# Node features loaded on 128 partitions in halves and quarters, and the node table stored in blocks of 512 nodes

## The chip, the cores and the metric

The kernel runs on one core of a Trainium2 chip. The metric is the device time of one launch in microseconds. The core has five instruction streams that matter here: PE (matrix products; PEld is its weight load), DVE (vector operations), ACT (activations and copies, and some DMA issues), POOL (GpSimd: here mostly DMA issues whose descriptors it writes itself, the indirect gathers among them) and SP (DMA issues only). Sixteen DMA engines move the data of all queues.

## The reference, cut to what matters

One layer of a graph network, with 12500 nodes of 160 features, 400000 edges sorted by destination, and a layer norm at the end. The 160 features of a node are 64 scalars and 32 vectors of 3 components.

```python
s = x[:, :64]; v = x[:, 64:].reshape(n, 32, 3); a = node_vec1
h_s = s @ lin1_ws * a / sqrt(64)                              # first maps: the table
h_v = einsum('nci,cd->ndi', v, lin1_wv) * a[:, :, None] / sqrt(32)
w = silu(edge_attr_64 @ fc_w1 / sqrt(64)) @ fc_w2 / sqrt(64)  # weights of an edge
es, ev = h_s[src], h_v[src]                                   # gather from the table
# products of es, ev with w and with edge_attr_4 (e0, e1): mid_s, mid_v
agg = segment_sum(mid, dst, n) / sqrt(16)
o = agg @ lin2 * a                                            # second maps
pre = self connection of x (sc_ws, sc_wv) + o
x = layernorm(x + gated(pre))
```

The change concerns the two lines of the first maps alone: how `x` comes into the core, how `h` is computed from it, and how `h` gets into the table in DRAM from which the edges gather.

## The kernel before, in words

The host lays the inputs out: `xs_t` is the 64 scalar features transposed (64 rows of 12500 nodes), `xv_t` the 96 vector components (three groups of 32 rows), `attr` the node attribute as 128 partitions by 98 columns (node = 128 x column + partition). The order of the instructions on each engine is that of the program (a manual schedule); engines wait for one another by semaphores only.

The start (lines 203 to 383). First come constants: an identity, iotas, memsets. `share`, an iota of 1040 numbers on POOL (L219), is needed only by `bases`, which derives the first node of each block of edges from the first row of `dst`. Then the node features are loaded in chunks of CH = 2048 nodes by `load` on SP (L233): `xa` holds the scalars in partitions 0 to 63 (L239) and two of the three vector components in 64 to 127 (L240), each a DMA of 64 rows of 8 KB; `xz` holds the third component (L245), as quarters: partition 4 c + q has component row c, quarter q of the chunk, so that 128 partitions hold 512 nodes each. There are six full chunks and a last one of 212 nodes. Between the loads ACT issues those of the weights, of the attribute (`at`, L265) and of the first row of `dst` (L268).

From the weights two matrices of 128 x 128 are built on DVE: `l1` has the scalar map and two copies of the vector map on its diagonal, `l1z` the vector map four times, spread so that rows of one quarter feed the columns of that quarter.

The loop over the chunks (L320): per chunk 16 matmuls (L331) turn 128 nodes each into 128 of the 160 features, with the features as the stationary operand; four at a time fill a PSUM bank (`hp`). DVE multiplies a bank with the attribute into `ht` (L334). Four more matmuls (L347) and one DVE product (L350) make the last 32 features of all 2048 nodes. After the fourth chunk begins, `bases` runs once on DVE (L309). At the end of a chunk POOL issues one DMA that stores 2048 rows of 640 bytes to the table `h_tab` (L361). `ht` has three buffers, so the fourth chunk's products wait for the first chunk's store. A matmul of fp32 shows as two records of PE.

After the loop: `lo` spreads the bases over the partitions with PE (L371). POOL issues, behind its stores, the edge features of the first chunk of edges (`es`, two DMAs, L372) and the whole of `dst` (`dt`, L373). SP issues, behind the last 84 rows' store (L364), the small weights of the later maps (L386, L297, L409), and then what the edge loop loads. When `dt` is there, DVE computes `rel`, each edge's destination less its block's base (L416, L421). Its PSUM is then free for the banks of the edge loop.

The edge loop (L874) takes 4 tiles of 128 edges a step, 3125 tiles in all. POOL gathers the source rows of each tile from `h_tab` with one indirect DMA (L468) into one of four buffers of four tiles (44 tiles are fetched by SP, row by row). PE computes the hidden layer (L459) and the weights of the edges (L510), DVE the products (L520, L528), PE sums them up by destination (L589), and further steps turn, map and add the sums. A buffer of gathered rows is free when the products of its step are done.

## Time and profile before

| | |
|---|---|
| median of 3 runs | 3964.24 us (3958.78 to 3966.85) |
| the profiled execution: its own time | 3954.57 us |
| its span | 3952.6 us |
| PE busy | 3649.2 us (92%) |
| POOL busy | 2929.3 us (74%) |
| DVE busy | 2415.6 us (61%) |
| ACT busy | 894.0 us (23%) |
| DMA traffic | 412.50 MB, 104 GB/s in the mean, 230 GB/s in the first of 40 slices |

The page gives the whole execution; the change lies in its first fortieth. So the useful answers are those for a window: the windows view gives for a stretch of time the busy time and the number of instructions of PE, PEld, DVE, ACT and POOL, the granted PE clock, the mean busy share of the DMA engines and their rate in GB/s. A line of the timeline has the start and the duration in us, engine, line, operation, what it writes and reads, how many instructions were merged, and in brackets how long the engine had been idle and what released it. In the list of groups stand the busy time and the mean in ns, and then the idle time before the group with its releasers. In the list of waits stand the total in us, how often, and the longest. A releaser is inferred, and where several were awaited it is the one that came last by the trace.

### The profile page before, as it was taken

The page shows a single profiled execution, that of the slowest core. Times are in us where ns is not written, and L with a number is a line of the kernel's source. Part 1 is how long each engine was busy: PE and PEld are TensorE (multiplying, and loading weights), DVE is VectorE, ACT ScalarE, POOL GpSimd, SP SyncE. Part 2 cuts the span into 40 slices and gives each one's busy share as a digit, 9 for nine tenths or more (in the row PEclk, how much of TensorE's full clock was granted, in tenths as well). Part 3 has the DMA queues.
Part 4 walks back from the last instruction along what each step waited for, and adds up shares of the span by engine and source line. Part 5 has one row for each costly group of instructions (what it writes and reads, how often), then busy time and mean ns, then how long its engine had stood idle before and what let it go on. Part 6 is the DMA issues. An engine that isn't in the chain of part 4 may idle for free. (4 is left out here: it accounts for less than half of the span.)

```text
span 3952.6 us, 58252 instructions
## 1 busy us (share of the span) xinstructions
PE 3649.2 (92%) x14269; PEld 1584.2 (40%) x14269; DVE 2415.6 (61%) x6524; ACT 894.0 (23%) x2480; POOL 2929.3 (74%) x3100
## 2 busy tenths in 40 slices
PE   5899999999999999999999999999999998999997
PEld 4343343343444344334344344344343443344343
DVE  5656565665665665656656656666665665666665
ACT  1322222222222222222222222222221221222222
POOL 4777777777777777777777777777777777777774
PEclk8999999999999999999999999999999999999999
DMA  8443444444444444344443443444443444444442
GB/s 230 97 103 90 108 105 96 108 103 105 100 96 110 103 97 108 95 116 96 102 110 86 110 110 89 108 100 100 108 106 90 109 103 105 100 100 108 100 109 55
DMA packets 243192, 412.50 MB, mean 104 GB/s; under 512 B 83069, under 2 KB 173497, under 8 KB 241945
## 3 DMA queue, kind: packets, MB, share of 16 engines
q0 software_dynamic: 150160, 262.93, 27.3%
q1 hardware_dynamic: 92246, 145.66, 15.8%
q8 instruction: 115, 1.88, 0.2%
q14 instruction: 235, 1.93, 0.2%
q10 hardware_dynamic: 436, 0.10, 0.0%
HBM read 392.43 MB, written 16.00 MB: 103 GB/s over the span
## 5 line engine op out<-in xcount | busy, mean ns | idle before, releaser
L468 POOL DMA_INDIRECT hg<-h_tab,idx x3081 | 2915.0, 946 | 949.5 <-issue 846.7
L510 PE MATMUL pw<-w,hid 128*128 128x448 f32 x3126 | 1363.3, 560 | 119.1 <-DVE sel L582 78.2
L589 PE MATMUL pa<-pr,sel 128*64 128x416 f32 x6250 | 1302.2, 539 | 3.1 <-DVE pw L573 2.9
L528 DVE TENSOR_TENSOR pr<-pw,hg 128x384 f32<-128x384 f32 x2313 | 1136.9, 547 | 0.0
L520 DVE TENSOR_TENSOR pr<-pw,hg 128x512 f32<-128x512 f32 x771 | 532.7, 691 | 876.8 <-DMA hg<-h_tab,idx 623.1
L510 PEld LDWEIGHTS pw<-w,hid 128*128 128x128 f32 x3126 | 555.2, 194 | 595.2 <-issue 461.6
L589 PEld LDWEIGHTS pa<-pr,sel 128*64 128x64 f32 x6250 | 388.0, 139 | 814.0 <-issue 803.6
L795 ACT COPY sa<-pa 128x416 f32<-128x416 f32 x521 | 263.3, 505 | 1205.7 <-PE pa L589 1190.5
L573 DVE TENSOR_TENSOR pw<-rel,iota 128x64 f32<-128x64 int16 x782 | 179.6, 230 | 543.5 <-PE pw L510 541.2
L459 PE MATMUL misc<-es,w 128*128 128x512 f32 (+1 forms) x784 | 450.2, 656 | 26.8 <-DVE rel L421 21.6
L461 ACT ACTIVATE hid<-misc 128x512 f32<-128x512 f32 x392 | 233.5, 596 | 778.4 <-PE misc L459 778.1
L598 PEld LDWEIGHTS misc<-ident,sa 128*128 128x128 f32 x2084 | 240.2, 141 | 318.7 <-issue 267.8
L613 PE MATMUL misc<-tt,l 128*96 128x256 f32 (+5 forms) x1474 | 343.6, 380 | 6.6 <-DVE y L659 6.0
L598 PE MATMUL misc<-ident,sa 128*128 128x128 f32 x2084 | 328.4, 280 | 8.3 <-DVE acc L776 3.8
L582 DVE TENSOR_TENSOR sel<-pw,eas 128x256 f32<-128x256 f32 x782 | 322.8, 413 | 0.0
L613 PEld LDWEIGHTS misc<-tt,l 128*96 128x96 f32 (+1 forms) x1474 | 225.2, 162 | 142.5 <-issue 73.9
L601 ACT COPY tt<-misc 128x192 f32<-128x192 f32 x521 | 164.7, 316 | 501.9 <-PE misc L598 482.6
L459 PEld LDWEIGHTS misc<-es,w 128*128 128x128 f32 x784 | 119.6, 192 | 293.8 <-issue 238.5
L621 DVE TENSOR_TENSOR acc<-acc,os 96x32 f32 x1042 | 194.6, 187 | 28.0 <-ACT os L616 9.6
L646 PE MATMUL misc<-ident,acc 96*128 96x96 f32 x196 | 36.6, 272 | 97.1 <-DVE pw L573 67.9
L603 ACT COPY tt<-misc 128x64 f32<-128x64 f32 x521 | 117.1, 225 | 0.0
L616 ACT COPY os<-misc 96x512 f32<-96x512 f32 (+2 forms) x67 | 38.2, 569 | 293.4 <-PE misc L613 286.7
(86 smaller groups left out, 608.6 us busy)
## 6 DMA issues: line engine op xcount, KB each, us to landing
es<-in_es_t_dram SPq DMA_DIRECT2D x258, 384.0 KB
hq<-h_tab SPq DMA_DIRECT2D x5632, 0.6 KB
hg<-h_tab,idx POOLq DMA_INDIRECT x3081
h_tab<-ht POOLq DMA_DIRECT2D x6, 1280.0 KB
xt<-in_x_dram SPq DMA_DIRECT2D x23, 320.0 KB
out_dram<-y SPq DMA_DIRECT2D x23, 320.0 KB
xv<-in_xv_t_dram SPq DMA_DIRECT2D x25, 187.5 KB
xs<-in_xs_t_dram SPq DMA_DIRECT2D x25, 125.0 KB
```

Of the source, the lines that this page charges most:

```text
L459: nc.tensor.matmul(ph[:k, c], w1[:k, :k], es[:k, t0 * P + c0 * P:t0 * P + c1 * P], start=True, stop=True)
L461: nc.scalar.activation(hid[:k, c], ph[:k, c], AF.Silu, scale=1.0 / math.sqrt(64))
L468: nc.gpsimd.indirect_dma_start(out=hg[:, t, :], out_offset=None, in_=h_tab, in_offset=bass.IndirectOffsetOnAxis(ap=i, axis=0))
L510: nc.tensor.matmul(pw[:, t:t + m, :NWT], hid[:m * S, c * P:(c + 1) * P], w2[:m * S, :m], start=True, stop=True)
L520: nc.vector.tensor_mul(two, pw[:, :n, :2 * S].rearrange("p t (k c) -> p t k c", k=2), hg[:, :n, None, :S].to_broadcast([P, n, 2, S]))
L528: nc.vector.tensor_mul(pr[:, :n, first:first + V3].rearrange("p t (i c) -> p t i c", i=3), pw[:, :n, None, 2 * S + k * V:2 * S + (k + 1) * ...
L582: nc.vector.tensor_mul(sel[:, :n], oh[:, :, None, :].to_broadcast([P, n, 4, W]), by_slot(tiles[0][0])[:, u:u + n, :, None].to_broadcast([P ...
L589: nc.tensor.matmul(pa[half * ROWS:(half + 1) * ROWS, :NPR], sel[:, t].rearrange("p k w -> p (k w)"), pr, start=start, stop=stop)
L598: nc.tensor.transpose(pt[:, four * P:four * P + k], sa[:k, c:c + P], ident[:k, :k])
L613: nc.tensor.matmul(po[:, k, :nb], l2[r, terms[to, part, four]], a[:, :nb], start=(n == 0), stop=(n == len(of) - 1))
L621: nc.vector.tensor_add(window, window, os[:, :, b])
L795: nc.scalar.copy(sa, pas.pop(j)[:, :NPR])
```

## The change

Each row of features is cut into halves and quarters of 3125 nodes per quarter, over all 12500 nodes. A chunk is now 512 columns of each quarter (again 2048 nodes), and the chunk that is left over (53 columns, 212 nodes) is the first one. `xw` holds the scalars and the first two vector components as two DMAs of 128 partitions each: partition 2 c + h has row c, half h, and in it two pieces, one for each quarter of that half. `xz` has partition 4 c + q as before, now with one piece of a quarter of the whole row. So `l1s` and `l1v` have the maps once for each half, and zero off the diagonal of the halves; `l1z` stays as it was.

A matmul with one piece of the scalars gives the scalar features of 128 nodes of two quarters, one with the components the vector features; four of them fill a bank for 4 x 128 nodes. Per chunk there are still 20 matmuls, the four of `xz` first now, and five DVE products. Each bank of 512 nodes is stored with a DMA of its own right after its product, from POOL: 24 stores of 512 rows and, for the left-over chunk, four of 53 rows, where there were six of 2048, one of 128 and one of 84 (on SP).

The attribute is needed in the new arrangement: `at_k` is loaded by seven small DMAs on POOL, ahead of `share`'s iota, which moves behind them. The weights are loaded with each row repeated for its halves or quarters (four DMAs on ACT for three), and `at` (now needed for `half_at` alone) behind the first row of `dst`.

```diff
--- before.py
+++ after.py
@@ -216,15 +216,15 @@
     nc.vector.memset(l2, 0.0)
     share = ends_pool.tile([1, NB], I32, name="share")
     even = NB // (2 * KB) * 2 * KB
-    nc.gpsimd.iota(share[:, :even], pattern=[[2 * KB * RATE, even // (2 * KB)], [RATE, KB], [KB * RATE, 2]],
-                   base=0, channel_multiplier=0)
-    nc.gpsimd.iota(share[:, even:], pattern=[[RATE, NB - even]], base=even * RATE, channel_multiplier=0)
 
     U = 4
     dt = ends_pool.tile([P, TT], I32, name="dt")
     base_f = ends_pool.tile([1, NB], F32, name="base_f")
-    CH = 4 * U * P
-    starts = list(range(0, N, CH))
+    assert N % 4 == 0
+    QN = N // 4
+    CH = U * P
+    starts = list(range(0, QN, CH))
+    starts = starts[-1:] + starts[:-1]
     with tc.tile_pool(name="nodes", bufs=len(starts)) as nodes, tc.tile_pool(
         name="nodes_ps", bufs=6, space=PSUM
     ) as nps, tc.tile_pool(name="z_ps", bufs=2, space=PSUM) as zps:
@@ -232,56 +232,71 @@
 
         def load(c0):
 
-            cn = min(CH, N - c0)
-            quarters = 4 if cn == CH else 1
-            assert quarters == 4 or cn <= U * P
-            xa = nodes.tile([P, CH], F32, name="xa")
-            nc.sync.dma_start(xa[:S, :cn], xs_t[:, c0:c0 + cn])
-            nc.sync.dma_start(xa[S:, :cn], xv_t[:2 * V, c0:c0 + cn])
-            xz = nodes.tile([P, U * P], F32, name="xz")
-            cq = cn // quarters
-            z = xv_t[2 * V:, c0:c0 + cq]
-            if quarters == 4:
-                nc.sync.dma_start(xz[:, :cq], bass.AP(tensor=z.tensor, offset=z.offset,
-                                                      ap=[[z.ap[0][0], V], [cq, 4], [1, cq]]))
-            else:
-                nc.sync.dma_start(xz[S:S + V, :cq], z)
-            loaded.append((c0, cn, quarters, cq, xa, xz))
+            cn = min(CH, QN - c0)
+            xw = nodes.tile([P, 2, 2, CH], F32, name="xw")
+            xz = nodes.tile([P, CH], F32, name="xz")
+            for k, m in enumerate((xs_t, xv_t)):
+                nc.sync.dma_start(xw[:, k, :, :cn],
+                                  bass.AP(tensor=m.tensor, offset=m[0:1, c0:c0 + 1].offset,
+                                          ap=[[2 * QN, P], [QN, 2], [1, cn]]))
+            z = xv_t[2 * V:2 * V + 1, c0:c0 + 1]
+            nc.sync.dma_start(xz[:, :cn], bass.AP(tensor=z.tensor, offset=z.offset,
+                                                  ap=[[QN, P], [1, cn]]))
+            loaded.append((c0, cn, xw, xz))
 
         load(starts[0])
 
-        def repeated(w, n, each):
-
-            return bass.AP(tensor=w.tensor, offset=w.offset,
-                           ap=[w.ap[0], [0, n], w.ap[1]] if each else [[0, n], *w.ap])
-
-        ws = ends_pool.tile([S, S], F32, name="ws")
-        nc.scalar.dma_start(ws, lin1_ws)
+        def spread(w, ap):
+
+            return bass.AP(tensor=w.tensor, offset=w.offset, ap=[*ap, [1, w.shape[1]]])
+
+        ws = ends_pool.tile([P, S], F32, name="ws")
+        nc.scalar.dma_start(ws, spread(lin1_ws, [[S, S], [0, 2]]))
         wv = ends_pool.tile([P, V], F32, name="wv")
-        nc.scalar.dma_start(wv[S:], repeated(lin1_wv, 2, False))
+        for i in range(2):
+            nc.scalar.dma_start(wv[i * S:(i + 1) * S], spread(lin1_wv, [[V, V], [0, 2]]))
         wz = ends_pool.tile([P, V], F32, name="wz")
-        nc.scalar.dma_start(wz, repeated(lin1_wv, 4, True))
-        at = consts.tile([P, NT], F32, name="at")
-        nc.scalar.dma_start(at, attr)
+        nc.scalar.dma_start(wz, spread(lin1_wv, [[V, V], [0, 4]]))
+
+        NQ = -(-QN // P)
+        at_k = ends_pool.tile([P, 4, NQ], F32, name="at_k")
+        for q in range(4):
+            t0, s = divmod(q * QN, P)
+            nc.gpsimd.dma_start(at_k[:P - s, q], attr[s:, t0:t0 + NQ])
+            if s:
+                m = min(NQ, NT - t0 - 1)
+                assert m == NQ or P - s >= QN - (NQ - 1) * P
+                nc.gpsimd.dma_start(at_k[P - s:, q, :m], attr[:s, t0 + 1:t0 + 1 + m])
+        nc.gpsimd.iota(share[:, :even], pattern=[[2 * KB * RATE, even // (2 * KB)], [RATE, KB], [KB * RATE, 2]],
+                       base=0, channel_multiplier=0)
+        nc.gpsimd.iota(share[:, even:], pattern=[[RATE, NB - even]], base=even * RATE, channel_multiplier=0)
         for c0 in starts[1:3]:
             load(c0)
         nc.scalar.dma_start(dt[0:1], dst[0:1])
+        at = consts.tile([P, NT], F32, name="at")
+        nc.scalar.dma_start(at, attr)
         for c0 in starts[3:]:
             load(c0)
 
-        l1 = consts.tile([P, P], F32, name="l1")
-        nc.vector.memset(l1, 0.0)
-        l1z = consts.tile([P, P], F32, name="l1z")
+        at_q = at_k.rearrange("p q b -> p b q")
+        l1s = consts.tile([P, 2, S], F32, name="l1s")
+        l1v = consts.tile([P, 2, 2, V], F32, name="l1v")
+        l1z = consts.tile([P, 4, V], F32, name="l1z")
+        halves = ends_pool.tile([P, 2], F32, name="halves")
+        sides = ends_pool.tile([P, 2, 2], F32, name="sides")
         quarter = ends_pool.tile([P, 4], F32, name="quarter")
+        nc.vector.tensor_reduce(halves, ident.rearrange("p (r h) -> p h r", h=2), AX.X, OP.add)
+        nc.vector.tensor_scalar_mul(halves, halves, 1.0 / math.sqrt(S))
+        nc.vector.tensor_mul(l1s, ws[:, None, :].to_broadcast([P, 2, S]),
+                             halves[:, :, None].to_broadcast([P, 2, S]))
+        nc.vector.tensor_reduce(sides, ident.rearrange("p (i r h) -> p h i r", i=2, h=2), AX.X, OP.add)
+        nc.vector.tensor_scalar_mul(sides, sides, 1.0 / math.sqrt(V))
+        nc.vector.tensor_mul(l1v, wv[:, None, None, :].to_broadcast([P, 2, 2, V]),
+                             sides[:, :, :, None].to_broadcast([P, 2, 2, V]))
         nc.vector.tensor_reduce(quarter, ident.rearrange("p (c q) -> p q c", q=4), AX.X, OP.add)
         nc.vector.tensor_scalar_mul(quarter, quarter, 1.0 / math.sqrt(V))
-        nc.vector.tensor_scalar_mul(l1[:S, :S], ws, 1.0 / math.sqrt(S))
-        for i in range(2):
-            r = slice(S + i * V, S + (i + 1) * V)
-            nc.vector.tensor_scalar_mul(l1[r, r], wv[r], 1.0 / math.sqrt(V))
-        nc.vector.tensor_mul(
-            l1z.rearrange("p (q c) -> p q c", q=4), wz[:, None, :].to_broadcast([P, 4, V]),
-            quarter[:, :, None].to_broadcast([P, 4, V]))
+        nc.vector.tensor_mul(l1z, wz[:, None, :].to_broadcast([P, 4, V]),
+                             quarter[:, :, None].to_broadcast([P, 4, V]))
         scales = []
 
         def scale(most):
@@ -317,51 +332,37 @@
             nc.vector.tensor_reduce(early, share, AX.X, OP.min)
             nc.vector.tensor_scalar(early, early, -float(MARGIN), None, op0=OP.is_lt)
 
-        for c0, cn, quarters, cq, xa, xz in loaded:
+        for c0, cn, xw, xz in loaded:
             if c0 == 3 * CH:
                 bases()
-            ht = nodes.tile([P, 4 * U, D], F32, name="ht", bufs=3)
-            nt = -(-cn // P)
-            first = c0 // P
-            full = cn // P
-            for t0 in range(0, nt, U):
-                ps = nps.tile([P, U, P], F32, name="hp")
-                for t in range(t0, min(t0 + U, nt)):
-                    n = min(P, cn - t * P)
-                    nc.tensor.matmul(ps[:n, t - t0], xa[:, t * P:t * P + n], l1,
-                                     start=True, stop=True)
-                k = min(U, full - t0)
+            ht = nodes.tile([P, U, 4, D], F32, name="ht", bufs=3)
+            pz = zps.tile([P, U, 4, V], F32, name="pz")
+            b0 = c0 // P
+            nb = -(-cn // P)
+            blocks = [slice(u * P, min(cn, (u + 1) * P)) for u in range(nb)]
+            n = min(cn, P)
+            assert all(c.stop - c.start == n for c in blocks)
+            for u, c in enumerate(blocks):
+                nc.tensor.matmul(pz[:n, u].rearrange("p q c -> p (q c)"), xz[:, c],
+                                 l1z.rearrange("p q c -> p (q c)"), start=True, stop=True)
+            nc.vector.tensor_mul(
+                ht[:n, :nb, :, P:], pz[:n, :nb],
+                at_q[:n, b0:b0 + nb, :, None].to_broadcast([n, nb, 4, V]))
+            for u, c in enumerate(blocks):
+                ps = nps.tile([P, 2, 2, 2, S], F32, name="hp")
+                for s in range(2):
+                    for k, m in enumerate((l1s.rearrange("p h c -> p (h c)"),
+                                           l1v.rearrange("p h i c -> p (h i c)"))):
+                        nc.tensor.matmul(ps[:n, :, s, k], xw[:, k, s, c], m, start=True, stop=True)
                 nc.vector.tensor_mul(
-                    ht[:, t0:t0 + k, :P], ps[:, :k],
-                    at[:, first + t0:first + t0 + k, None].to_broadcast([P, k, P]))
-                if t0 + k < nt <= t0 + U:
-                    n = cn - full * P
-                    nc.vector.tensor_scalar(ht[:n, full, :P], ps[:n, full - t0],
-                                            at[:n, first + full:first + full + 1], None, op0=OP.mult)
-
-            pz = zps.tile([P, U, 4, V], F32, name="pz")
-            r = slice(0, P) if quarters == 4 else slice(S, S + V)
-            by = l1z if quarters == 4 else l1[r, r]
-            for u in range(-(-cq // P)):
-                n = min(P, cq - u * P)
-                nc.tensor.matmul(pz[:n, u, :quarters].rearrange("p q c -> p (q c)"),
-                                 xz[r, u * P:u * P + n], by, start=True, stop=True)
-            if quarters == 4:
-                nc.vector.tensor_mul(
-                    ht[:, :, P:].rearrange("p (q u) c -> p u q c", q=4), pz,
-                    at[:, first:first + 4 * U].rearrange("p (q u) -> p u q", q=4)[:, :, :, None]
-                    .to_broadcast([P, U, 4, V]))
-            else:
-                nc.vector.tensor_mul(ht[:, :full, P:], pz[:, :full, 0],
-                                     at[:, first:first + full, None].to_broadcast([P, full, V]))
-            if cn > full * P:
-                n = cn - full * P
-                nc.vector.tensor_scalar(ht[:n, full, P:], pz[:n, full, 0],
-                                        at[:n, first + full:first + full + 1], None, op0=OP.mult)
-            nc.gpsimd.dma_start(
-                h_tab[c0:c0 + full * P, :].rearrange("(q p) d -> p q d", p=P), ht[:, :full])
-            if cn > full * P:
-                nc.sync.dma_start(h_tab[c0 + full * P:c0 + cn, :], ht[:n, full])
+                    ht[:n, u, :, :P], ps[:n].rearrange("p h s k c -> p (h s) (k c)"),
+                    at_q[:n, b0 + u, :, None].to_broadcast([n, 4, P]))
+                to = h_tab.rearrange("(q r) d -> r q d", q=4)[c0 + u * P:c0 + u * P + n]
+                if n == P:
+                    nc.gpsimd.dma_start(to, ht[:, u])
+                else:
+                    for q in range(4):
+                        nc.gpsimd.dma_start(to[:, q], ht[:n, u, q])
 
 
     lo_ps = ends.enter_context(tc.tile_pool(name="lo_ps", bufs=1, space=PSUM))
```

## The prediction, made before the result was known

> **What bounds the kernel now.** I read the page first: PE is the busiest engine (92%), and POOL, at 74%, looks like an engine with room. Its group in the table of costliest lines and its waits after the start say otherwise.
>
> ```profile
> span 3952.6 us, 58252 instructions
> L468 POOL DMA_INDIRECT hg<-h_tab,idx x3081 | 2915.0, 946 | 949.5 <-issue 846.7
> ```
>
> Next I asked for the groups of POOL alone from 85 to 3920 us, its waits from 85 us on, and the timeline at both ends of the gathers.
>
> ```profile
> L468 POOL DMA_INDIRECT hg<-h_tab,idx x3065 | 2899.8, 946 | 937.4 <-issue 842.1 <-DMA hg<-h_tab,idx 25.9 <-DVE pr L528 18.4
> POOL hg L468 <- issue: 842.1, 2763, 0.3
> 80.15 0.95 POOL L468 DMA_INDIRECT hg<-h_tab,idx  x1 [0.30 <-issue]
> 84.58 0.94 POOL L468 DMA_INDIRECT hg<-h_tab,idx  x1 [3.48 <-DVE pr L528]
> 3917.34 0.94 POOL L468 DMA_INDIRECT hg<-h_tab,idx  x1 [0.30 <-DVE pw L573]
> ```
>
> POOL issues one gather per tile of 128 edges, busy 0.946 us with a fixed 0.30 us ahead. (3917.34 - 84.58) / 3064 = 1.251 us per gather: from the 17th gather at 84.58 to the last POOL waits for nothing longer than that 0.30. So the end is the start of the 17th gather, plus 3064 x 1.251, plus a tail of 35 us. Nothing after 84.58 is touched by the change, and what the change saves or costs is the shift of that one instruction. What sets it is read from the timeline of the start:
>
> ```profile
> 53.17 0.58 POOL L373 DMA_DIRECT2D dt<-in_dst_dram  x1
> 61.30 1.04 POOL L468 DMA_INDIRECT hg<-h_tab,idx  x1 [7.55 <-DMA scv<-in_sc_wv_dram]
> 69.16 6.24 DVE L416 TENSOR_TENSOR rel<-dt,lo 128x260 int16<-128x260 int32 x12 [15.63 <-DMA dt<-in_dst_dram]
> 75.83 2.05 PE L459 MATMUL misc<-es,w 128*128 128x512 f32 x2 [21.65 <-DVE rel L421]
> 78.56 3.35 PE L510 MATMUL pw<-w,hid 128*128 128x448 f32 x4 [0.69 <-ACT hid L461]
> 82.22 0.69 DVE L520 TENSOR_TENSOR pr<-pw,hg 128x512 f32<-128x512 f32 x1
> ```
>
> Gathers can begin when the last row of the table has landed (61.30; the releaser named there is a small load, but the table's stores are what a gather reads). Four buffers of four tiles let 16 gathers run, to 81.1; the 17th needs the first products. Those hang on another chain: dt (the destinations, 1562.5 KB) is issued on POOL behind all stores of the table, lands at 69.16, and rel, the hidden layer, the weights and the products follow, 84.58 - 69.16 = 15.4 us. This chain ends 3.5 us after the gathers' own. Both follow the end of the stores. The start in stages, with the DMA engines' share and rate as the last two columns:
>
> ```profile
> 0.00:5.00 5.00, 0.00 (x0) 0.00 (x0) 3.94 (x9) 0.64 (x1) 4.38 (x8) 1.00 0.60 129
> 5.00:10.00 5.00, 0.70 (x3) 0.71 (x4) 0.84 (x4) 0.64 (x1) 0.36 (x2) 1.00 1.07 216
> 10.00:15.00 5.00, 5.00 (x26) 5.00 (x26) 1.85 (x4) 0.00 (x0) 0.00 (x0) 1.00 1.02 218
> 15.00:20.00 5.00, 4.89 (x44) 4.73 (x44) 3.53 (x6) 0.00 (x0) 1.39 (x1) 1.00 0.98 201
> 20.00:25.00 5.00, 3.34 (x30) 3.18 (x29) 2.50 (x4) 0.00 (x0) 1.19 (x1) 1.00 1.06 220
> 25.00:26.00 1.00, 1.00 (x11) 1.00 (x10) 0.71 (x2) 0.00 (x0) 0.00 (x0) 1.00 0.88 234
> 26.00:30.00 4.00, 2.83 (x26) 2.67 (x25) 3.49 (x6) 0.00 (x0) 1.12 (x1) 1.00 1.02 382
> ...
> 55.00:60.00 5.00, 0.00 (x0) 0.00 (x0) 0.00 (x0) 0.00 (x0) 0.00 (x0) 0.50 1.00 265
> 60.00:65.00 5.00, 0.00 (x0) 0.00 (x0) 0.00 (x0) 0.00 (x0) 2.95 (x3) 0.50 1.02 231
> 65.00:66.00 1.00, 0.00 (x0) 0.00 (x0) 0.00 (x0) 0.00 (x0) 0.83 (x1) 0.50 1.02 419
> ```
>
> From 5 to 65 us the DMA share is 1.0 in every window asked for: the start is bound by transfers. But a full share is not one rate. While only node features load (5 to 25) it is about 215 GB/s; once stores run beside the loads, 382; at 65, with dt (128 partitions) alone, 419. The first stage loads mostly in halves of 64 partitions.
>
> **The change part by part.** ```profile
> xa<-in_xs_t_dram SPq DMA_DIRECT2D x6, 512.0 KB
> dt<-in_dst_dram POOLq DMA_DIRECT2D x1, 1562.5 KB
> es<-in_es_t_dram POOLq DMA_DIRECT2D x2, 384.0 KB
> ```
>
> *Loads.* Each 512 KB of features now lies on 128 partitions instead of 64, in pieces of 2 KB instead of 8 KB. The windows from 5 to 25 moved (216 + 218 + 201 + 220) x 5 = 4.28 MB in 20 us. At 380, the rate of the mixed stage with its 2 KB quarters, they take 11.3: -8.7 us. The ends: nothing gained (the quarters were on 128 partitions in 2 KB pieces before, and the window 5 to 10, which holds a quarter load, still shows 216), and -9.8 at dt's 419. I take 380, which is nearer to dt's row, as dt is the one load of 128 whole rows. Loads after 26 us run beside stores at that rate already and gain nothing.
>
> [...]
>
> *Start.* The 212 left-over nodes load first (136 KB), with about 115 KB of weights and attributes. The fourth load on SP waits for an earlier one, and that wait now falls where little is queued:
>
> ```profile
> SPq L239 <- DMA ws<-in_lin_ws_dram: 3.8, 1, 3.8
> 6.39 0.49 SPq L239 DMA_DIRECT2D xa<-in_xs_t_dram  x1
> ```
>
> Before, 129 x 5 + 216 = 0.86 MB had moved by 6 us; now some 0.25 will have. 0.61 MB at 380 is +1.6 us of lost transfer. Ends: 0 (ws lands with nothing ahead of it, and chunk 1 loads at once) and +2.5 (the small loads drag).
>
> *Tail.* Now the last pieces are a full chunk:
>
> ```profile
> 46.47 1.06 PE L347 MATMUL pz<-l1z,xz 128*128 128x128 f32 x8
> 35.89 3.81 PE L331 MATMUL hp<-l,xa 128*128 128x128 f32 x32 [2.16 <-DMA xa<-in_xv_t_dram]
> L334 DVE TENSOR_TENSOR ht<-hp,at 128x512 f32<-128x512 f32 (+1 forms) x25 | 16.0, 671 | 14.5 <-DMA h_tab<-ht 7.9 <-PE hp L331 6.6
> 11.41 0.69 DVE L334 TENSOR_TENSOR ht<-hp,at 128x512 f32<-128x512 f32 x1 [0.43 <-PE hp L331]
> 17.72 1.39 POOL L361 DMA_DIRECT2D h_tab<-ht  x1 [12.36 <-DVE ht L350]
> 45.83 1.15 POOL L361 DMA_DIRECT2D h_tab<-ht  x1 [6.28 <-DVE ht L350]
> 49.96 1.15 POOL L361 DMA_DIRECT2D h_tab<-ht  x1 [2.98 <-DVE ht L350]
> 51.55 0.57 POOL L361 DMA_DIRECT2D h_tab<-ht  x1 [0.44 <-DVE ht L359]
> POOL h_tab L361 <- DVE ht L350: 38.4, 6, 12.4
> 74.03 1.12 SPq L200 DMA_DIRECT2D es<-in_es_t_dram  x2
> ```
>
> From its landing to its last store's bytes lie 1.06 (z) + 3.81 (blocks) + 0.67 (DVE) + 0.57 (issue) + about 1.5 for descriptors (between 0.6 and 1.9, below), 7.6 us. To fill them the DMA has three of the chunk's four stores (0.98 MB, 2.6 us) and what is left of the chunk before (0 to 4 us). So it idles between 1 and 5 us; I take +2, nearer to the low end, as some of that store will be left. Before, the last full store had been issued 1.6 us ahead of 51.55, and the share after it stayed at 1.0: no idle.
>
> *Stores.* 28 on POOL instead of 7, with the one on SP gone. POOL waits 38 us for DVE in this stage, so the issue is hidden: 24 x 0.57 to 1.15 is 14 to 28 us of 40. What descriptors cost behind the issue is bounded from above by the last two full stores: both were issued from 45.83 and had landed at 61.30, so 4096 rows took under 15.5 us, 1.9 us per 512. From below by the issue itself, 0.57. I take 1.2, between, which is covered (a chunk's four stores, 4.8 us, in PE's 4.9); at 1.9 the cover is gone and that is the second rival.
>
> *Order of queues.* Seven small attribute loads come ahead of share's iota on POOL; DVE needs them for its first product (11.41 before), and 7 x 0.57 from about 1.5 ends near 5.5. If they are late, DVE starts some us later, under loads that keep the DMA busy: 0. On SP the tail store, which sat behind DVE, goes; the 24 small weight loads move up, and with them the second chunk of es (2 x 384 KB, at 74.03 before), which could come in beside dt: 0 to 3.6 us (0.79 MB at 216). I take 0, as it stood 5 us behind dt's landing and both move. On ACT one more weight load is issued, and at goes behind dt's first row, where only half_at needs it: 0. The maps built by DVE (nine operations instead of seven, 0.2 to 0.3 us each) lie under the loads.
>
> *Matrix work.* 20 matmuls per chunk before and after, of the same 128 x 128 x 128; DVE has five products of 512 columns per chunk as before: 0. If the DMA no longer covers it, PE's six chunks of 4.9 us from 11 end at 40, still ahead of the stores.
>
> Sum: -8.7 + 1.6 + 2 = -5.1 us on the end of the stores, hence on dt, rel and the 17th gather: the span goes from 3952.6 to 3947.5. That execution's own time was 3954.57, 0.24% below the median of the runs (3964.24); applied to the median the forecast is 3959.1 us. A difference under 0.2% (8 us, the spread of the three runs) is about what a measurement of this kernel cannot tell from no change.
>
> **The rivals.** *The idle closes.* If the SP wait ends early and the DMA has leftovers through the tail, only the loads' term stands, -8.7, down to -9.8, and the dt and es loads may gain a little more as the small weights are out of their way: 3955, faster. For it: share 1.0 in every window of the start. Against: a small chunk at the front leaves nothing queued.
>
> *The descriptor generator on POOL becomes the bound.* One mechanism, at the stores. The first store was issued at 17.72, and the rate rises only between the windows 25 and 26, some 8 us later, for 2048 rows. If a DMA costs POOL's generator what a gather's pitch shows, 1.25 us for 128 rows, and further rows at (8.3 - 1.25) / 1920 = 3.7 ns, a 512-row store costs 2.7 us. 24 of them are 64 us from about 13 (the first product at 11.41 and one block): the stores end at 77 instead of 60. The bound of 1.9 holds where a large store shares the fixed part; between the two, at 2.3, they end at 68: +8, 3972, slower. It decides from (60 - 13) / 24 = 1.95 us per store. Against it: 382 GB/s with stores in the mix at 26 to 30.
>
> [...]
>
> *The loads don't get faster.* The 2 KB pieces stay at about 216 GB/s, as the quarters' window suggests. Then the first term is 0; the stores begin earlier and take transfer time out of the load-only stage, which pays for the start and tail: about +1, 3965.
>
> **How the numbers follow.** Forecast (-2 to -9 us, 3955 to 3962 by itself): 0.45, of it 0.14 beyond 8 us. Idle closes: 0.26. Loads stay slow: 0.12. Generator: 0.17. Faster by over 0.2%: 0.14 + 0.26 = 0.40; within: 0.31 + 0.12 = 0.43; slower: 0.17. The range goes from 3950 (the idle closes, es and dt gain 2 us more, and a median lies 3 us low, as far as the runs of before spread) to 3971 (just under the generator's middle price), and leaves out some 2 in 10: the generator's dearer half and a gain beyond 14 us.
>
> **What would show it.** In the changed profile: windows between 6 and 14 us at 350 GB/s or more while only features load; a first store before 15 us; the last table store's issue near 46; the first gather near 56, rel near 64 and the 17th gather near 79.5, then 1.25 us per gather with no other wait. The start term is seen as a dip of the DMA share below 0.7 between 3 and 6, the tail term as a dip between the last load and the first es. The generator would show as gaps between store packets with DVE waiting for stores while the share is under 0.8. The forecast is wrong if the load windows stay near 216, if gathers change their pitch, or if rel is held by something other than dt.

## The result, and the profile after

The changed kernel takes 3957.32 us in the median (3955.72 to 3959.18), the kernel before, run beside it, 3965.98 us (3958.78 to 3968.15). The ratio is 0.998 with a 95% interval of 0.9973 to 0.9987: 8.7 us less, between 5.2 and 10.7. Of the runs below, `load_forms`, `loads_alone`, `blocks_alone`, `leftover_last` and `act_stores` fell on chips on which the kernel before itself takes some 5300 us, so their times are set only against the kernel before on the same chip, while their starts, whose load rates are those of the profiles here, are set against the other starts.

The profiled execution hides this. The page after shows a longer span than the page before (3956.8 against 3952.6 us):

```profile
span 3956.8 us, 58315 instructions
L469 POOL DMA_INDIRECT hg<-h_tab,idx x3081 | 2923.8, 949 | 949.9 <-issue 831.7
```

One gather took 949 ns in this execution and 946 in that of before. Over 3064 gathers that is 9 us, and it does not belong to the change: in two later profiles, below, both kernels have the same pitch. So the spans of single profiles are not compared here, but the instant at which the steady pitch begins. The timeline of the changed kernel (start, duration, engine, line, idle time and releaser in brackets):

```profile
13.21 2.10 POOL L365 DMA_DIRECT2D h_tab<-ht  x4 [3.71 <-DVE ht L357]
16.91 3.43 POOL L362 DMA_DIRECT2D h_tab<-ht  x4 [1.59 <-DVE ht L357]
34.37 5.97 POOL L362 DMA_DIRECT2D h_tab<-ht  x8 [4.73 <-DVE ht L357]
43.77 0.75 POOL L362 DMA_DIRECT2D h_tab<-ht  x1 [0.73 <-DMA h_tab<-ht]
46.08 0.57 POOL L374 DMA_DIRECT2D dt<-in_dst_dram  x1 [0.40 <-DMA h_tab<-ht]
52.61 1.05 POOL L469 DMA_INDIRECT hg<-h_tab,idx  x1 [5.96 <-DMA scv<-in_sc_wv_dram]
61.12 6.25 DVE L417 TENSOR_TENSOR rel<-dt,lo 128x260 int16<-128x260 int32 x12 [16.80 <-DMA dt<-in_dst_dram]
77.32 0.96 POOL L469 DMA_INDIRECT hg<-h_tab,idx  x1 [4.86 <-DVE pw L574]
3919.40 0.94 POOL L469 DMA_INDIRECT hg<-h_tab,idx  x1 [0.30 <-issue]
```

Against the rows of before: the last store is issued 7.8 us earlier, the first gather starts 8.7 us earlier, rel 8.0, the 17th gather 7.3. Nothing is lost up to rel; the last step gives back 0.7. The windows of the changed kernel (PE, PEld, DVE, ACT, POOL busy; PE clock; DMA share; GB/s):

```profile
0.00:3.00 3.00, 0.00 (x0) 0.00 (x0) 1.93 (x8) 0.00 (x0) 2.24 (x10) 1.00 0.16 31
3.00:6.00 3.00, 0.00 (x0) 0.00 (x0) 1.86 (x7) 0.75 (x1) 3.00 (x6) 1.00 0.81 152
6.00:14.00 8.00, 4.18 (x19) 3.84 (x19) 4.70 (x4) 0.53 (x1) 4.29 (x4) 1.00 1.04 374
...
10.00:15.00 5.00, 5.00 (x23) 4.65 (x23) 1.66 (x3) 0.00 (x0) 1.79 (x4) 1.00 1.05 387
15.00:20.00 5.00, 5.00 (x44) 5.00 (x43) 3.27 (x5) 0.00 (x0) 3.05 (x5) 1.00 1.05 391
20.00:25.00 5.00, 5.00 (x48) 5.00 (x47) 3.79 (x7) 0.00 (x0) 3.36 (x5) 1.00 1.05 400
...
40.00:45.00 5.00, 4.22 (x26) 3.00 (x24) 3.64 (x17) 0.00 (x0) 3.83 (x6) 1.00 1.01 311
45.00:50.00 5.00, 0.05 (x1) 0.00 (x0) 0.00 (x0) 0.00 (x0) 1.19 (x3) 0.65 0.97 277
```

From 6 to 20 us, while nearly only features load, the DMA engines move 374 to 391 GB/s where they moved 201 to 220 (in the window from 20 to 25 half of the changed kernel's bytes are already stores). The first 6 us are poorer than before, whose windows were:

```profile
0.00:3.00 3.00, 0.00 (x0) 0.00 (x0) 1.97 (x8) 0.00 (x0) 2.38 (x8) 1.00 0.31 57
3.00:6.00 3.00, 0.00 (x0) 0.00 (x0) 2.27 (x2) 1.28 (x1) 2.37 (x2) 1.00 1.04 240
```

Bytes by 6 us: 31 x 3 + 152 x 3 = 0.55 MB after, 57 x 3 + 240 x 3 = 0.89 MB before. At 391 GB/s the missing 0.34 MB are 0.9 us.

### The profile page after: what moved, and what is told of

It is laid out like the page before. It is cut to its first block, busy times and chain, and to the rows that moved or that the text cites. A ratio compares the mean times of both kernels' runs of the same rounds, so it can differ in the third digit from the quotient of the medians.

```text
span 3956.8 us, 58315 instructions
## 1 busy us (share of the span) xinstructions
PE 3645.0 (92%) x14271; PEld 1580.1 (40%) x14271; DVE 2418.3 (61%) x6524; ACT 895.1 (23%) x2480; POOL 2954.4 (75%) x3128
## 5 line engine op out<-in xcount | busy, mean ns | idle before, releaser
L622 DVE TENSOR_TENSOR acc<-acc,os 96x32 f32 x1042 | 196.5, 189 | 29.6 <-ACT os L617 11.3
```

The lines of the kernel that those rows point to most:

```text
L622: nc.vector.tensor_add(window, window, os[:, :, b])
```

## The experiments

**What makes a load slow.** The changed kernel with six groups of loads ahead of its own, each of 4 x 512 KB into a spare tile, and a small DVE copy that waits for the group. Forms: as after (128 partitions, two pieces of 2 KB), 128 partitions of 4 KB, 64 of 8 KB as before's `xa`, 64 in four pieces of 2 KB, the layout of before's quarters (32 rows in four pieces, here of 4 KB), 128 equal rows of 4 KB.

```diff
...
+        group(1, lambda k: nc.sync.dma_start(
+            probe[:, k, :1024], rows_of_x(xs_t, 0, 1024 * k, [[2 * QN, P], [1, 1024]])))
+        group(2, lambda k: nc.sync.dma_start(
+            probe[:S, k], rows_of_x(xs_t, 0, 2048 * k, [[N, S], [1, 2048]])))
...
+        group(4, lambda k: nc.sync.dma_start(
+            probe[:, k, :1024], rows_of_x(xv_t, 2 * V, 512 * k, [[N, V], [QN, 4], [1, 1024]])))
...
```

> The changed kernel with six groups of loads ahead of it, each group done before the next begins, four DMAs of 512 KB per group into a scratch tile that no product uses: (0) 128 partitions x two pieces of 2 KB, (1) 128 partitions x one piece of 4 KB, (2) 64 partitions x one piece of 8 KB, (3) 64 partitions x four pieces of 2 KB, (4) 128 partitions x 4 KB, but read from DRAM as 32 rows of four quarters, as the old quarter loads were, (5) 128 partitions x 4 KB of the same rows read as 128 equal rows. If the rate hangs on the number of partitions (my theory), groups 0, 1 and 5 take near 2.1 MB / 390 = 5.4 us plus some 2 us of latency, groups 2 and 3 near 9.8 plus 2, and 4 shows whether the old quarters shared the slow rate for another reason. If it hangs on the size of a piece (rival: the loads don't get faster), 2 is the fastest, 0 and 3 are alike and slower. If it hangs on neither, all take the same.

The timeline of the second to the fifth group, and a window from the middle of the second and of the third; a group begins at its SP line and ends where the DVE copy starts:

```profile
10.65 1.80 SPq L264 DMA_DIRECT2D probe<-in_xs_t_dram  x4
18.32 0.17 DVE L259 COPY seen<-probe 128x4 f32<-128x4 f32 x1 [7.70 <-DMA probe<-in_xs_t_dram]
18.52 2.44 SPq L266 DMA_DIRECT2D probe<-in_xs_t_dram  x4
31.34 0.17 DVE L259 COPY seen<-probe 128x4 f32<-128x4 f32 x1 [12.85 <-DMA probe<-in_xs_t_dram]
31.54 2.52 SPq L268 DMA_DIRECT2D probe<-in_xs_t_dram  x4
44.49 0.17 DVE L259 COPY seen<-probe 128x4 f32<-128x4 f32 x1 [12.98 <-DMA probe<-in_xs_t_dram]
44.69 1.76 SPq L271 DMA_DIRECT2D probe<-in_xv_t_dram  x4
52.41 0.17 DVE L259 COPY seen<-probe 128x4 f32<-128x4 f32 x1 [7.75 <-DMA probe<-in_xv_t_dram]
...
13.00:16.00 3.00, 0.00 (x0) 0.00 (x0) 0.00 (x0) 0.00 (x0) 0.00 (x0) 1.00 1.02 419
21.00:28.00 7.00, 0.00 (x0) 0.00 (x0) 0.00 (x0) 0.00 (x0) 0.00 (x0) 1.00 1.04 213
```

2.1 MB take 7.67 us on 128 partitions and 12.82 on 64; in four pieces instead of one, 64 partitions take 12.95. Between these forms the number of partitions decides, and on 64 partitions the size of the piece does not. The rates in the middle are 419 and 213 GB/s, at a DMA share of 1.02 and 1.04. At these rates the bytes take 5.0 and 9.8 us, so some 2.7 and 3.0 us of a group lie outside the steady rate, where the expectation put some 2. The layout of quarters took 7.72, as fast as 128 rows, so what was slow in the window of 216 that held a quarter load must have been the halves beside it. The first group, in the form of the changed kernel, is no fair comparison: it ran at the very start, beside other loads, and took 9.70 us. The sixth took 7.89, with the kernel's own loads already queued behind it. For pieces of 2 KB on 128 partitions the evidence is the changed kernel itself, 387 GB/s from 10 to 15.

It also bears on before's way of loading both halves of the partitions, scalars on 0 to 63 and vectors on 64 to 127, one right behind the other (the first two issues at 0.75 and 1.39 us): its windows from 5 to 25 us show 201 to 220 GB/s, and one half alone moves 213 here. So the second half added nothing that these rates show; why not is open.

**The loads without the rest, the stores without the rest.** Both were run twice. The edge loop of these runs has no fixed pitch (in `loads_alone` POOL waits 1308.3 us for DVE's products between 100 and 5200 us), so it is their starts that count.

`loads_alone`: the changed kernel with the left-over chunk last, and the four stores of a chunk together behind its last product. A store still has 512 rows, so what is taken away is that it starts early, and the place of the left-over chunk.

```diff
-    starts = starts[-1:] + starts[:-1]
...
+            for q in range(4):
+                to = h_tab[q * QN + c0:q * QN + c0 + cn]
                 if n == P:
-                    nc.gpsimd.dma_start(to, ht[:, u])
+                    nc.gpsimd.dma_start(to.rearrange("(u p) d -> p u d", p=P), ht[:, :, q])
```

> The new layout of the loads and the maps alone: the left-over chunk is last again, and each chunk is stored only after all of its products. My theory (the rate of the loads carries the gain): load-only windows at 380 to 400 GB/s, the 17th gather at 77 to 80 us (84.58 before, 77.32 in the changed kernel), time 5 to 8 us under the kernel before. Rival (early stores in blocks carry it): 17th gather at 82 or later, gain under 3 us.

> After, but with the left-over chunk last and the four stores of a chunk issued together once all its products are done. Theory (the loads carry the gain): 17th gather near 76, as in the changed kernel, 10 to 12 us ahead of the kernel before (87.2 in its last profile), ratio to before 0.9965 to 0.9985, i.e. 6 to 14 us less. Rival (the store per block carries part of it): 17th gather at 79 or later and a ratio of 0.9985 or more.

`blocks_alone`: the kernel before with its own loads, the products of the third component moved ahead of the others, and a store behind each bank.

```diff
             for t0 in range(0, nt, U):
...
+                if k:
+                    nc.gpsimd.dma_start(
+                        h_tab[c0 + t0 * P:c0 + (t0 + k) * P, :].rearrange("(q p) d -> p q d", p=P),
+                        ht[:, t0:t0 + k])
...
-            nc.gpsimd.dma_start(
-                h_tab[c0:c0 + full * P, :].rearrange("(q p) d -> p q d", p=P), ht[:, :full])
```

> The kernel before with its old loads, but the quarter products first in each chunk and a store of 512 rows after each bank. My theory: the load-only windows stay near 215 GB/s until the stores begin, now near 15 us instead of 26; from there the mixed rate; the total of bytes is the same, so that the stores end only some 2 to 5 us earlier, by the shorter load-only stage: 17th gather at 80 to 83. Rival (blocks carry the whole gain): 17th gather at 77. Rival (28 DMAs cost POOL's generator more than it has): later than 84.6.

> Before, with its loads of halves, but the quarter products first and a store for every 512 nodes. Theory (stores by block are worth nothing while the loads leave the DMA full): 17th gather within 2 us of before's (84.6 to 87.2), ratio 0.999 to 1.001. Rival (the rewritten products and stores bring gain of their own): 17th gather 3 us or more earlier and a ratio of 0.9990 or less. Generator theory: slower by 4 us or more, 17th gather at 90 or later.

Second runs, the loads alone (a window, and the first and 17th gather):

```profile
10.00:15.00 5.00, 5.00 (x24) 5.00 (x25) 1.38 (x2) 0.00 (x0) 0.00 (x0) 1.00 1.04 382
53.83 1.04 POOL L468 DMA_INDIRECT hg<-h_tab,idx  x1 [2.21 <-DMA h_tab<-ht]
77.98 0.95 POOL L468 DMA_INDIRECT hg<-h_tab,idx  x1 [4.32 <-DVE l L303]
```

and the stores by blocks alone:

```profile
10.00:15.00 5.00, 3.84 (x21) 3.85 (x22) 1.62 (x5) 0.00 (x0) 0.00 (x0) 1.00 1.06 214
62.05 1.03 POOL L469 DMA_INDIRECT hg<-h_tab,idx  x1 [5.73 <-DMA scv<-in_sc_wv_dram]
86.40 0.94 POOL L469 DMA_INDIRECT hg<-h_tab,idx  x1 [4.30 <-DVE pr L529]
```

The 17th gather came at 76.49 and 77.98 with the loads alone (77.32 in the changed kernel), and at 85.65 and 86.40 with the blocks alone (84.58 in the kernel before, 87.16 in its later profile). The ratios to the kernel before: loads 0.998 (0.9952 to 1.0007) and 0.9978 (0.9957 to 0.9998), blocks 0.9997 (0.9975 to 1.0018) and 1.0008 (0.9991 to 1.0025). With the loads alone nearly the whole shift is there, within 2 us of what was expected; with the blocks alone there is none. The first expectation for the blocks, 80 to 83, missed. Their first store is issued at 16.16 us instead of 17.72, but from 15 to 20 us the queue of the stores moves no byte, and from 20 to 25 only 0.18 of 1.07 MB (the first store, and the queue's packets, MB and share of the engines from 20 to 25):

```profile
16.16 0.98 POOL L361 DMA_DIRECT2D h_tab<-ht  x1 [10.79 <-DVE ht L353]
q0 software_dynamic: 41, 0.18, 14.8%
```

In the kernel before, too, the stores' first bytes move 7 to 8 us after the first issue (17.72, and the window from 25 to 26). Until then the loads' queue alone takes the engines' whole time there (102.7% from 17.7 to 25 us). Why the stores wait so long was not tried. This does not make early stores worthless in the changed kernel: `leftover_last`, next, differs from `loads_alone` only in its stores, one of each bank right after its product, and its 17th gather comes 2.4 us earlier on the one chip (74.10 against 76.49) and 4.1 us on the other (73.91 against 77.98). So beside loads at the full rate (381 to 385 GB/s from 10 to 15 us in these four runs) the early stores do carry a part.

**The left-over chunk last.** One line of the changed kernel less, run twice:

```diff
-    starts = starts[-1:] + starts[:-1]
```

> The changed kernel with the 212 left-over nodes last instead of first. If their place in front only costs an emptier DMA in the first 5 us and spares nothing at the end, the 17th gather comes within 1 us of 77.3. If a full chunk at the end had cost an idle tail (the tail term of the prediction, 2 us), it comes at 75 to 76.

> After with the left-over chunk of 212 nodes loaded and stored last instead of first. My start term (left-over first costs 0 to 2.5 us and the tail 1 to 5 if a full chunk ends): first gather 1 to 2 us ahead of the changed kernel's 52.5, 17th near 74 to 75, ratio to before about 0.9968, 1 to 2 us under the changed kernel. Rival (a full chunk in the tail would idle the DMA but a left-over in the tail costs its own fixed times): no earlier than the changed kernel, ratio 0.9972 to 0.998.

The second run (a window of the tail, and the 17th gather):

```profile
45.00:50.00 5.00, 1.56 (x6) 0.72 (x4) 0.76 (x7) 0.00 (x0) 3.41 (x7) 0.70 0.90 246
73.91 0.95 POOL L468 DMA_INDIRECT hg<-h_tab,idx  x1 [3.67 <-DVE pw L573]
```

The 17th gather came at 74.10 and 73.91, 1.8 to 3.4 us ahead of the changed kernel's (77.32 and, below, 75.88). The first expectation, 75 at the earliest, missed to the good side; the second, 74 to 75, nearly came. Part of it is seen in the first 5 us: 157 and 150 GB/s here, 60 and 52 in the two profiles of the changed kernel, which makes some 0.5 MB or 1.2 us at 391 GB/s. The rest was not broken down: the tail has a dip here (0.90), the first profile of the changed kernel has none (0.97), and the second has a deeper one (0.79, below). The ratio, 0.9985 (0.9964 to 1.0007), cannot tell this from the changed kernel.

**The same two kernels again, side by side.** No edit.

> The kernel before, unchanged, for a second trace of its start: if the start is as regular as I take it to be, the first gather is near 61.3, rel near 69.2 and the 17th gather near 84.6 us. The pitch of the later gathers can differ by some ns, as the two profiled executions of before and after did (1.251 and 1.254 us).

> The changed kernel, unchanged, for a second trace: first gather near 52.6, rel near 61.1, 17th gather near 77.3 us. The 1.1 us between the end of the first products and the 17th gather, which the kernel before did not show, appears again if it belongs to the program, and not if it is chance.

The expectation for before, 84.6, missed by 2.6 us; that of the 1.1 us came. The kernel before (a window, its 17th and its last gather):

```profile
25.00:30.00 5.00, 3.81 (x35) 3.62 (x33) 3.91 (x7) 0.00 (x0) 1.11 (x2) 1.00 0.99 222
87.16 0.94 POOL L468 DMA_INDIRECT hg<-h_tab,idx  x1 [3.19 <-DVE pr L528]
3921.12 0.95 POOL L468 DMA_INDIRECT hg<-h_tab,idx  x1 [0.30 <-issue]
```

and the changed one (two windows, PE's wait for the last chunk, and the same two gathers):

```profile
40.00:45.00 5.00, 5.00 (x26) 5.00 (x25) 2.02 (x3) 0.00 (x0) 0.75 (x1) 0.50 0.87 305
45.00:50.00 5.00, 3.62 (x19) 2.35 (x18) 2.82 (x16) 0.00 (x0) 3.90 (x6) 1.00 0.79 238
38.84 2.08 PE L346 MATMUL pz<-l1z,xz 128*128 128x128 f32 x8 [3.10 <-DMA xz<-in_xv_t_dram]
75.88 0.95 POOL L469 DMA_INDIRECT hg<-h_tab,idx  x1 [3.59 <-DVE pw L574]
3910.19 0.95 POOL L469 DMA_INDIRECT hg<-h_tab,idx  x1 [0.30 <-DVE pw L574]
```

The pitch is (3921.12 - 87.16) / 3064 = 1.251 and (3910.19 - 75.88) / 3064 = 1.251 us: equal. The 17th gather moved by 11.3 us, the last by 10.9, the time by 11.9 (3959.46 to 3947.6). In this pair what the start saves arrives at the end. The kernel before was 2.6 us later here than in its first profile because its slow stage lasted longer: its window of 25 to 30 still shows 222, where the first profile had begun to mix in stores (382 from 26 on).

**dt ahead of es.** As dt's chain releases the 17th gather, dt is issued first:

```diff
-    load_chunk(0, nc.gpsimd)
     nc.gpsimd.dma_start(dt, dst)
+    load_chunk(0, nc.gpsimd)
```

> The changed kernel with one edit: POOL issues dt ahead of the first es instead of behind it. If the chain dt, rel, hidden layer, products sets the 17th gather (my theory), dt lands about 0.79 MB at 215 GB/s = 3.7 us earlier, near 57.5, and the 17th gather comes near 73.5, then limited by the first gather + 20. If the gathers' own start sets it (rival), it stays near 77.

Two windows and two lines of the timeline:

```profile
50.00:55.00 5.00, 0.00 (x0) 0.00 (x0) 0.00 (x0) 0.00 (x0) 2.93 (x3) 0.50 0.99 318
55.00:60.00 5.00, 0.00 (x0) 0.00 (x0) 0.70 (x2) 0.00 (x0) 2.50 (x4) 0.50 1.00 169
59.30 6.23 DVE L417 TENSOR_TENSOR rel<-dt,lo 128x260 int16<-128x260 int32 x12 [12.59 <-DMA dt<-in_dst_dram]
75.48 0.95 POOL L469 DMA_INDIRECT hg<-h_tab,idx  x1 [1.36 <-DVE pw L574]
```

rel starts 0.4 us earlier than beside it (59.68), the 17th gather 0.4: missed. The one run took 3950.34 us, 2.7 more than the one of the changed kernel beside it. The rate falls from 318 to 169 GB/s while dt's last packets are still out (rel starts at 59.30); es (64 partitions, 64 x 1536 elements), issued from 46.83 us on, is in flight then: a wait of POOL for it ends at 61.70. That es shares the engines with the rest of dt is a reading of these windows and was not tried by itself.

**The stores on ACT's queue.** The table's stores, es and dt are issued by ACT instead of POOL.

```diff
-                    nc.gpsimd.dma_start(to, ht[:, u])
+                    nc.scalar.dma_start(to, ht[:, u])
...
-    load_chunk(0, nc.gpsimd)
-    nc.gpsimd.dma_start(dt, dst)
+    load_chunk(0, nc.scalar)
+    nc.scalar.dma_start(dt, dst)
```

> After, but the table's stores, the first es and dt are issued on ACT's queue instead of POOL's. If POOL's descriptor generator or its issue holds the stores back (rates of 217 to 311 between 40 and 55 us in the changed kernel), the last store lands 3 us or more earlier, first gather at 49.5 or before and 17th at 73 or before. If the DMA engines themselves are the limit: first gather within 1.5 us of 52.5, 17th within 2 us of 76 to 77.

A window and three lines of the timeline:

```profile
20.00:25.00 5.00, 5.00 (x47) 5.00 (x46) 2.07 (x3) 0.00 (x0) 0.00 (x0) 1.00 0.70 200
19.49 35.58 ACTq L362 DMA_DIRECT2D h_tab<-ht  x24
26.57 0.69 DVE L348 TENSOR_TENSOR ht<-pz,at_k 128x512 f32<-128x512 f32 x1 [4.10 <-DMA h_tab<-ht]
83.80 0.95 POOL L469 DMA_INDIRECT hg<-h_tab,idx  x1 [5.38 <-DVE pr L529]
```

Neither expectation came: it is later, by 5.9 us at the first gather (58.55) and 6.5 at the 17th. The share falls to 0.70, DVE waits 4.10 us for a store to free a buffer, and that is the picture that the prediction gave for POOL's generator as the bound, only on ACT's queue. Why the stores fare worse there was not settled. What POOL spends on the stores is not what limits the changed kernel in any way that this move relieves.

**All that helped, together.** The left-over chunk last, dt ahead of es, and of `bases` only the copies of the first row of dst stay in the middle of the chunks, its arithmetic (some 3 us of DVE) comes after the last chunk:

```diff
-    starts = starts[-1:] + starts[:-1]
...
+        def spans():
+
             nc.vector.tensor_copy(base_f, rows)
...
+        spans()
...
-    load_chunk(0, nc.gpsimd)
     nc.gpsimd.dma_start(dt, dst)
+    load_chunk(0, nc.gpsimd)
```

> The changed kernel with the left-over chunk last, dt ahead of es, and of bases only the three copies after the fourth chunk, the other four operations (3.5 us of DVE) after the last chunk. If the start alone sets the time and its three parts add up, the 17th gather comes at 70 to 72 us and the time is 12 to 15 us under that of the kernel before, 5 to 7 under that of the changed one. If the order at the end is already limited by the DMA, it comes at 74, as with the left-over chunk last alone.

Its 16th and 17th gather:

```profile
69.09 0.95 POOL L472 DMA_INDIRECT hg<-h_tab,idx  x1 [0.30 <-issue]
71.15 0.95 POOL L472 DMA_INDIRECT hg<-h_tab,idx  x1 [1.11 <-DVE pw L577]
```

3945.85 us (3945.01 to 3946.88) against 3958.45 for the kernel before beside it: ratio 0.9967 (0.9955 to 0.9979), 12.6 us less. The 17th gather and the gain over the kernel before came as expected; the gain over the changed kernel, expected at 5 to 7 us, did not, as its one run beside it took 3947.6, 1.8 more than this median. From the changed kernel's second profile to this one the 17th gather moved by 4.7 us, the last gather by 4.0 (3910.19 to 3906.18), and the end of the span by 2.2 (3945.8 to 3943.6): the stretch behind the last gather took 37.4 us here and 35.6 there. rel starts at 55.00, and of POOL's wait ahead of the 17th gather 1.1 us are left: dt's chain is nearly as early as the gathers themselves, so the next microsecond would have to come from the end of the stores, which was not tried.

## Why the prediction was right, and where its terms were off

**The time, 3959.1 us.** The median came at 3957.32, inside the range, and the direction is faster. The shift was forecast as -5.1 us and measured as -8.7 (-10.7 to -5.2). The forecast lies just outside that interval; the middle is the rival in which the idle closes (-8.7 to -9.8, 3955), to which the prediction gave 0.26. So the direction and the loads' term were foreseen, and that the median lies within 2 us of 3959.1 is partly luck: the kernel before came out 1.7 us slower than the median the forecast was applied to.

**The bound: right, but looser than it was put.** The end follows the start of the 17th gather, and between the two later profiles that start and the last gather moved together (11.3 and 10.9 us), at an equal pitch. The tail, put at 35 us, is not fixed: it took 35.3 and 36.4 in the two profiles of before, 37.4 and 35.6 in those of the changed kernel, 37.3 with dt first and 37.4 in the last experiment. A gain of 2 us at the start can be lost in it, and the single pair of profiles first shown would have misled further, by 3 ns on each gather.

**Loads, -8.7: right, in mechanism and size.** At (387 + 391) / 2 = 389 GB/s, the windows from 10 to 20 us in which nearly only features load, the 4.28 MB of the first stage take 11.0 us instead of 20: -9.0. The number of partitions was the cause, as the experiment with the six forms showed. The lower end, nothing gained, rested on the window that held a quarter load and still showed 216; it was a mixed window. The upper end took 419 GB/s as dt's alone, though gathers ran beside it from 61.30 on; the experiment's 419 bears the number out. That the share is 1.0 in every window from 5 to 65 us is not quite so (0.88 from 25 to 26). In `load_forms` 64 partitions have half the rate of 128, 213 against 419 GB/s.

**Start, +1.6: mis-sized, +0.9.** The dip is there (0.16 from 0 to 3 us, 0.81 from 3 to 6), less deep than the 0.7 that was named for 3 to 6, and the fourth load on SP was not held up: the wait for ws had ended when SP came to it, and the chunk behind the left-over was issued from 3.03 us on.

**Tail, +2: the idle came in one of two profiles.** In the first the share stays at 0.97 and above from 6 to 50 us. There `bases` holds DVE, POOL waits 4.73 us until 34.37 and then issues eight stores in a row; a backlog of stores lies behind the loads and covers the last chunk's products: from 40 to 44 us, while DVE makes the last three of them, the stores' queue moves 1.23 MB and alone takes 99.5% of the engines' time. In the second profile the same eight stores are issued, from 32.60, and the idle comes all the same: the share is 0.87 and 0.79 from 40 to 50 us, which is (0.13 + 0.21) x 5 = 1.7 us. PE gets the last chunk's xz only at 38.84 and works through the chunk until 46.5, at a granted clock of 0.50 for most of it, where the prediction counted 4.9 us; the last store is issued at 47.5. That is the prediction's picture, and near its size. But it does not show at the gathers: rel and the 17th gather come 1.4 us earlier in the second profile than in the first, and from 40 to 60 us both moved about the same bytes, 5.7 MB. What the idle costs is therefore open, and so is the sum of the terms. With the start as measured and no tail it is -9.0 + 0.9 = -8.1, against -7.8 at the last store and -8.7 at the first gather; but the kernel before itself shifted by 2.6 us between its two profiles, more than either small term.

**Stores hidden: right.** Eight stores in a row took 5.97 us of issue, 0.75 each, and the 24 lie between 16.91 and 44.52: at most 1.15 us per store with all waits (1.39 in the second profile, from 14.99 to 48.27), against 1.95 from which, by the prediction's estimate, the generator would have decided. POOL's part in its DMAs is seen in the profile as busy time: its issues are instructions of POOL itself (0.75 us a store, 0.949 us a gather), while those of SP and ACT stand on SPq and ACTq, and its queue q0 bears the kind software_dynamic, that of the feature loads, q1, hardware_dynamic. A generator of descriptors behind the issue is in no view; what it would cost was the author's estimate from the instants of issue and landing. The 24 were issued within 28 us and had landed when the first gather began at 52.61, and with before's loads stores of 320 KB cost nothing measurable against those of 1.25 MB (ratios 0.9997 and 1.0008).

**Loads stay slow, 3965: refuted** by the windows.

**The marks.** First store 13.21 (before 15 forecast; a store of the left-over rows, the first of 512 rows comes at 16.91), last 43.77 (46), first gather 52.61 (56), rel 61.12 (64), 17th gather 77.32 (79.5): all early, the last four by 2.2 to 3.4 us; start and tail stood in the sum with 2.7 us more than this profile shows. In the second profile the last store came later than the mark (47.5), the first gather at 52.46 and the 17th at 75.88.

**rel to the 17th gather, 15.4 us: 16.2 after.** In the changed kernel the last product that frees the buffers ends at 76.3 and the gather starts 1.05 us later, behind DVE's next weight product; in the kernel before it starts 0.27 us after it. It repeats: 1.05 to 1.06 in the changed kernel's second profile, with the loads alone, with the left-over chunk last, with dt first and in the last experiment, and 0.26 to 0.27 in the kernel before's second profile, with the blocks alone and with the stores on ACT. It belongs to the program and not to chance; what the gather waits for there is open. It costs some 0.8 us.

## What to carry to other kernels

A DMA share of 1.0 did not tell the rate here: 1.02 stood beside 419 GB/s and 1.04 beside 213. Compare the GB/s of windows with equal share, and where one is half of another, look at how many partitions the transfers in it cover. Laying transfers of 512 KB over 128 partitions instead of 64 doubled the rate, from 213 to 419 GB/s, and the changed kernel kept 387 of it with pieces of 2 KB. Starting stores earlier was worth nothing beside loads at 214 to 217 GB/s, and 2 to 4 us at the 17th gather beside loads at 381 to 385, so a part that gains nothing alone can still gain with the other. Find the one instruction behind which the rest runs at a fixed pitch, and judge a change to the start by its shift, over several profiles, since the span of one profile can be off by more than the gain and the start of one kernel by 2.6 us.

## What the runs showed that was not expected

- The pitch of 3081 like gathers differs between executions by up to 3 ns each (946 in before and 949 in the changed kernel, which has 947 in its second profile), which is 9 us of the span and as much as the whole gain.
- The 24 stores lie between 16.91 and 44.52 us when POOL issues them (0.75 us each in the median) and between 19.49 and 55.07 on ACT's queue (0.91 us in the median, 2.30 at most; the rest is time between them), with the DMA share down at 0.70 from 20 to 25 us.
- Pieces of 2 KB were no slower than rows of 8 KB on 64 partitions (12.95 and 12.82 us for 2.1 MB), and the changed kernel's 128 partitions reach 387 to 391 GB/s with them.
